# Passing from attention to the experts: the expert counts' own PSUM bank, weight splits moved behind the masked copies, the second item's rows turned earlier, and the second expert cut into items of 2 and 4 tiles

## The chip, the cores and the metric

The program runs on one core of one Trainium2 chip. Its engines are TensorE (PE, with its weight loads shown apart as PEld), VectorE (DVE), ScalarE (ACT), GpSimd (POOL) and SyncE (SP, which here only issues transfers). Each engine works through its own queue in order, and semaphores tie the queues together. The metric is the device time of one execution in microseconds (us), as the median of several runs.

## The reference, cut to what matters

A block of a transformer on 4096 tokens of width 256: a layer norm with modulation, windowed attention (16 heads of 64, window 128), a gated residual, a second modulated layer norm, and a mixture of experts with top-2 routing, 8 experts of width 1024 and a capacity of 640 rows per expert and choice.

```python
h = _layernorm(x) * (1 + ca) + sa
x = x + ga * attention(h, Wqkv, Wout)          # window of 128 keys, 16 heads
h = _layernorm(x) * (1 + cb) + sb
probs = softmax(h @ gate_w.T + gate_b);  topk_prob, topk_idx = top_k(probs, 2)
for c in range(2):                              # each choice
    pos = cumsum(one_hot(topk_idx[:, c]))[own] - 1
    keep = pos < 640                            # capacity
    xb = rows of h, put to slot (expert, pos)
    yb = relu(xb @ W1 + b1) @ W2 + b2           # per expert
    y += yb[slot] * prob * keep
x = x + gb * y
```

All of it is float32. The kernel keeps that precision by splitting each operand into a high and a low part in a reduced format and adding three products (`passes`, line 227).

## The kernel before, in words

**Attention.** The tokens are taken in 16 groups of 256 (`NG`), and the heads in 8 pairs. A software pipeline (`iteration(w)`, line 1084, for w = 0 to 66) does two head pairs in each step: scores of step w, softmax of step w-1, transposes (`turn`, `unpack`) and value products of step w-2, output projection of step w-3. On all five engines the order of instructions is exactly the order in which the program text emits them (`tc.manual_schedule`, line 1157). Within an iteration there are named places, in this order: A, B, M, H, C (ahead of the scores), S (after the scores' masked copies, `pack`), V (after the value products). Side work is hung on these places: the string "2B" in a list means "two iterations after the base, at place B".

**Close.** When a group's projection is complete, `close(g)` (line 633) does the residual, the second norm, the routing, and puts the rows into their slots in a DRAM buffer `xbuf` with four indirect transfers from POOL (line 819, "puts"). It is a generator of eleven pieces: 1 residual, 2 statistics, 3 the normed rows `h` (two adders on POOL, or on DVE for the last group), 4 transposes `tp_f`, 5 logits `pl`, 6 and 7 the two picks (7 ends with the running counts `pref`), 8 the position counts `cnt`, 9 weights, 10 ranks, 11 slot numbers and the puts. `CLOSE`, `LATE` (lines 1031 to 1036) say where each piece of a group is hung. In the last two groups (14 and 15) piece 8 also computes the rows an expert has so far (`totals`, line 737), by a matmul into free columns of the same PSUM bank as `cnt`. From it comes `shift`, which pushes the late rows of experts 0 and 1 behind row `EARLY` = 512, so that the rows ahead of it can be read back before the late puts are done.

**Experts.** The rows of an expert are in tiles of 128, ten tiles per expert at most. An item is a run of tiles of one expert: expert 0 has items 0 to 4 with 2 tiles each; expert 1 has item 5 with 4 tiles and items 6 to 8 with 2; then an item of 6 tiles and two of 2 for each further expert. For an item, `load_slots` reads rows from `xbuf` by a transfer on SP (line 870); `turn_slots` transposes them on PE (`tp_x`, line 895) and splits them on ACT and DVE into `xT` (line 127); `first_layer` and `second_layer` are the matmuls `ph` and `y` for each of 8 slices f of the hidden width, with `hm` made from `ph` by one ACT and two DVE instructions (lines 937 to 939); `y` runs two slices behind. `results` and `give` add the rows into the output by indirect transfers (line 1003). Weights of an expert come in four pieces (`Expert.steps`): load, then a split on ACT and DVE (`we`, line 127).

**The passage.** Items 0, 1, 5 and 2 bridge the two parts. Item 0 (expert 0) is woven into iterations 62 to 66. Item 1 follows with the last pieces of close(15) between its slices. Then comes item 5, which covers the time until the last puts are in DRAM and read back for item 2. Item 2 is the first that the tile scheduler orders itself. After it, items 3 and 4 run only if expert 0 has more rows than 6 tiles (`further`, a branch on all engines), then item 6, then items 7 and 8 under the same kind of branch, then item 9 with 6 tiles of expert 2. With these inputs expert 0 keeps 675 rows and expert 1 keeps 686, so items 3, 4, 7 and 8 are skipped.

The side work that the change touches was hung so:

```python
NG - 3: ["0H", "1A", "1B", "2B", "2H", "3A", "3B", "3H", "3C", "3C", "3C"],      # group 13
NG - 2: ["0H", "1A", "1B", "2B", "2H", "2C", "3A", "3B", "3M", "3C", "3C"],      # group 14
place(experts[0].pieces, NW - 4, "0A 2B 2C 3B 3C".split())     # NW = 64
place(experts[1].pieces, NW - 1, "0B 1B 1C 2M 3A".split())
place(first, NW - 2, "0A 1H 1S 2B 2H 2V 3B 3H 3V 4A".split())  # item 0
```

Of the kernel before, what the change touches and what calls it, by code (L numbers as in the profile page):

```python
# [8 lines left out]
FP = mybir.dt.float32  # L9
FR = mybir.dt.float32r  # L10
I32 = mybir.dt.int32
AF = mybir.ActivationFunctionType
ALU = mybir.AluOpType
# [4 lines left out]
P = 128  # L18
# [10 lines left out]
def adaln_block_kernel(  # L29
# [18 lines left out]
    nc = tc.nc  # L48
# [4 lines left out]
    E, _, FF = w1.shape  # L53
    CAP = 640
    KC = 2
    BUF = KC * CAP
    NSLOT = E * BUF
    T = B * S
    NT = T // P
    ND = D // P  # L60
    NP = H // 2
    NF = FF // P
    NB = BUF // P
    SBT = 2
    NG = NT // SBT
# [2 lines left out]

    EARLY = 4 * P
    WIDE = 6
    QSCALE = DH ** -0.5

# [16 lines left out]
    def bank(name, shape=(P, 512)):  # L91
        return ring["pool"].tile(list(shape), FP, tag="ring", name=name, bufs=ring["bufs"])
# [7 lines left out]
    ones = const.tile([P, P], FP, name="ones")  # L100
# [5 lines left out]
    shift = const.tile([P, 2], FP, name="shift")  # L106
# [215 lines left out]
    first = norm(0)  # L322
# [310 lines left out]
    def close(g):  # L633
# [3 lines left out]
        j0 = g * SBT  # L637
# [96 lines left out]
        n = SBT * KC * E  # L734
        ohf = oh.rearrange("p t k e -> p (t k e)")

        def totals(j, o):

            nc.tensor.matmul(
                out=cnt[:, o : o + KC * E], lhsT=ones,  # L740
                rhs=pref[:, j, :, :].rearrange("p k e -> p (k e)"), start=True, stop=True,
            )
            both = small.tile([P, KC, E], FP, tag="both", name=f"both_{g}_{o}", bufs=2)
            nc.vector.tensor_scalar(
                both.rearrange("p k e -> p (k e)"), cnt[:, o : o + KC * E], float(CAP), None, ALU.min
            )
            total = small.tile([P, E], FP, tag="total", name=f"total_{g}_{o}", bufs=2)
            nc.vector.tensor_tensor(total, both[:, 0, :], both[:, 1, :], ALU.add)
            return total

        if late:

            e = g - (NG - 2)
            total = totals(j0, n)
            nc.vector.tensor_scalar(
                shift[:, e : e + 1], total[:, e : e + 1], -1.0, float(EARLY), ALU.mult, ALU.add
            )
            nc.vector.tensor_scalar(shift[:, e : e + 1], shift[:, e : e + 1], 0.0, None, ALU.max)
        nc.tensor.matmul(out=cnt[:, 0:n], lhsT=tri, rhs=ohf, start=True, stop=False)
        nc.tensor.matmul(  # L760
            out=cnt[:, 0:n], lhsT=ones,
# [2 lines left out]
        )  # L764
        counts = small.tile([P, n], FP, tag="counts", name=f"counts_{g}", bufs=2)
        nc.vector.tensor_copy(counts, cnt[:, 0:n])
        yield
        sm = tile2("sm")
        nc.vector.tensor_reduce(sm, ex, AX.X, ALU.add)
# [32 lines left out]
        nc.vector.tensor_scalar(over, rank, float(CAP), float(2 * NSLOT), ALU.is_ge, ALU.mult)  # L802
        rows_of = NSLOT
        if late:
            rows_of = NSLOT - EARLY
            for e in range(g - (NG - 2) + 1):
                sel = tile2("sel", SBT * KC)
                nc.vector.tensor_scalar(
                    sel, pk, float((E - e) * P), shift[:, e : e + 1], ALU.is_equal, ALU.mult
                )  # L810
                nc.vector.tensor_tensor(pos_, pos_, sel, ALU.add)
# [19 lines left out]
                placed.append(put)  # L831
        if g == NG - 1:

            total = totals(NT, n)
            nc.vector.tensor_tensor(total[:, 0:2], total[:, 0:2], shift, ALU.add)
            nc.vector.tensor_copy(fill, total)

# [3 lines left out]

    items = []
    for e in range(E):
        head = 2 if e == 0 else 4 if e in (1, E - 1) else WIDE
        ends = [0, *range(head, NB + 1, 2)]
        items += [(e, range(lo, hi)) for lo, hi in zip(ends, ends[1:])]
    NI = len(items)
    xts, xTs, hms, yps, b2s = {}, {}, {}, {}, {}
# [28 lines left out]
    def turn_slots(q, n0):  # L877

        tiles = items[q][1]
        if n0 == 0:  # L880
            w = len(tiles)
            if q and (w > 2 or items[q - 1][0] in (1, E - 1) and items[q - 1][1].start == 0):
                w = WIDE
            xTs[q] = [
                (mp if q else early).tile([P, ND, w * P], FR, tag=f"xT{i}{w}", name=f"xT{i}_{q}")
                for i in range(2)
            ]
        m = min(2, len(tiles) - n0)
        if m <= 0:
            return  # L890
        tp = bank(f"tp_x{q}_{n0}")
        tpv = tp.rearrange("p (d s) -> p d s", d=ND)
        for n in range(m):
            for d in range(ND):
                turned = nc.tensor.transpose(
                    tpv[:, d, n * P : (n + 1) * P], xts[q][:, n0 + n, d * P : (d + 1) * P], ident
                )
                if q > 6:
                    tc.keep_in_program_order(turned)
        s = slice(n0 * P, (n0 + m) * P)  # L900
        split(xTs[q][0][:, :, s], xTs[q][1][:, :, s], tpv[:, :, 0 : m * P])
# [96 lines left out]
    def give():  # L998
# [31 lines left out]
    NORM = ["0B", "1A", "1H", "2A", "2B"]  # L1030
    CLOSE = ["0H", "1A", "1B", "2H", "3H", "4A", "4B", "5H", "6A", "6B", "6C"]
    LATE = {
        NG - 3: ["0H", "1A", "1B", "2B", "2H", "3A", "3B", "3H", "3C", "3C", "3C"],
        NG - 2: ["0H", "1A", "1B", "2B", "2H", "2C", "3A", "3B", "3M", "3C", "3C"],
        NG - 1: ["0H"],
    }
    places = {}
# [1 line left out]
    def place(work, w, at):  # L1039
        for a in at:  # L1040
            places.setdefault((w + int(a[0]), a[1]), []).append(work)
# [28 lines left out]

    experts = {e: Expert(e) for e in range(2)}
    first = first_item()
    place(experts[0].pieces, NW - 4, "0A 2B 2C 3B 3C".split())
    place(experts[1].pieces, NW - 1, "0B 1B 1C 2M 3A".split())
    place(first, NW - 2, "0A 1H 1S 2B 2H 2V 3B 3H 3V 4A".split())

    def go(w, at):
        for work in places.pop((w, at), ()):
            next(work, None)
# [4 lines left out]
    def iteration(w):  # L1084
        g, p2 = divmod(w, NP // 2)
        if p2 == NP // 2 - 1 and g + 2 < NG:
            xs[g + 2] = load_x(g + 2)
        for i in range(2 * w - 2, 2 * w):
            if 0 <= i < E:
                clear(i)  # L1090
        new, old, turned, done = pair(w), pair(w - 1), pair(w - 2), pair(w - 3)

        ahead = [divmod(i, NP // 2) for i in range(w + 1, NW if w == NW - 3 else w + 2) if i < NW]
        if w == NW - 2:
            ahead = []
        if w == NW - 2:
            project_v(g, 1, 1)
        if turned[0]:
            turn(*turned[0])
            unpack(*turned[0])  # L1100
        if old[0]:
            normalize(*old[0])
        go(w, "A")
        q = [project_qk(*a, 0) for a in ahead[:1]]
        if old[1]:
            exps(*old[1], [0])
        for a in q:
            part(*a)
        if turned[1]:
            turn(*turned[1])  # L1110
        if old[1]:
            exps(*old[1], [1, 2])
        if turned[1]:
            unpack(*turned[1])
        if old[1]:
            exps(*old[1], [3])
        go(w, "B")
        k = [project_qk(*a, 1) for a in ahead[:1]]
        if old[1]:
            normalize(*old[1])  # L1120
        for a in k:
            part(*a)
        for a in ahead[1:]:
            for i in range(2):
                part(*project_qk(*a, i))
        if done[0]:
            out_project(*done[0])
        if w < NW:
            for a in VALUES[p2] if g + 1 < NG else LAST_VALUES[p2]:
                project_v(g, *a)  # L1130
        go(w, "M")
        if done[1]:
            out_project(*done[1])
        go(w, "H")
        go(w, "C")
        for u in new:
            if u:
                scores(*u)
        if new[0]:
            pack(*new[0])  # L1140
            maximum(*new[0])
            pack(*new[1])
        go(w, "S")
        if turned[0]:
            values(*turned[0])
        if new[0]:
            maximum(*new[1])
            exps(*new[0], [0, 1])
        if turned[1]:
            values(*turned[1])  # L1150
        if new[0]:
            exps(*new[0], [2, 3])
        go(w, "V")

    part(*project_qk(0, 0, 1))
    everything = {mybir.EngineType.PE, mybir.EngineType.Activation, mybir.EngineType.DVE, mybir.EngineType.Pool, mybir.EngineType.SP}
# [4 lines left out]

    next(last)
    next(first)
    next(last)
    next(first)
    next(first, None)
# [4 lines left out]
    mp = ctx.enter_context(tc.tile_pool(name="moe", bufs=2, reuse_waits="tile"))  # L1171
    pm_ = ctx.enter_context(tc.tile_pool(name="pmoe", bufs=1, space=PSUM, reuse_waits="tile"))
    ring.update(pool=pm_, bufs=2)
    load_slots(1)
    load_slots(5)
    load_b2(1)
    turn_slots(1, 0)
    second = layers(1)
    for f in range(NF + LAG + 1):
        next(second, None)  # L1180
        next(last, None)
        if f in (6, 8):
            turn_slots(5, f - 6)
    load_slots(2, 2)
    load_slots(6, 2)
    third = layers(5)
    for f in range(NF + LAG + 1):
        next(third, None)
        if f == 0:
            give()  # L1190
        if f == 6:
            turn_slots(2, 0)
    order.__exit__(None, None, None)

# [24 lines left out]
    def do(f, *a):  # L1219
        return lambda: f(*a)  # L1220
# [24 lines left out]
                further(q + 1)  # L1245

    filled = []
    item(2, {0: [give], 3: [fills], 4: [do(turn_slots, 6, 0)], 6: [do(turn_slots, 3, 0)]})
    further(3)
    more = {f: [do(piece, 2)] for f in (0, 2, 4, 6)}  # L1250
    more[1] = [do(load_slots, 9)]
    more[7] = [do(turn_slots, 7, 0)]
    for i in range(3):
# [43 lines left out]
```

## Time and profile before

| what | value |
|---|---|
| median of 3 runs | 1161.58 us (1160.19 to 1163.09) |
| profiled execution, its own time | 1161.56 us |
| its span in the trace | 1159.8 us |
| PE busy | 1086.3 us (94%) |
| DVE busy | 877.4 us (76%) |
| ACT busy | 676.7 us (58%) |
| POOL busy | 593.8 us (51%) |
| mean granted TensorE clock | 0.97 |

The page's second part cuts the span into 40 slices of 29 us each and gives a digit for every engine, tenths of busy time. Its row PEclk is the clock granted to TensorE in the same tenths. In a timeline each row is a run of like instructions: start, duration, engine, line and operation, the tile written and those read, the count, and in brackets how long the engine was idle just before and which instruction or transfer released it.

### The profile page before, as it was taken

How to read it: one execution, taken by the hardware profiler on the slowest of the kernel's cores; microseconds unless marked ns; L12 is line 12 of the kernel's file. 1: busy time of each engine (PE TensorE's matmuls, PEld its weight loads, DVE VectorE, ACT ScalarE, POOL GpSimd, SP SyncE). 2: the span in 40 equal slices, each digit the busy share in tenths (PEclk: the TensorE clock that was granted, in tenths of full speed). 3: DMA queues.
4: the chain of work that ended last, by engine and by line, in shares of the span. 5: the costliest groups of instructions: out<-in, count | busy, mean ns of one | idle time of the engine just before them, and what ended most of it. 6: DMA issues, size and time to landing. Idle time of an engine off the chain costs nothing. (4 is left out here: it accounts for less than half of the span.)

```text
span 1159.8 us, 25187 instructions
## 1 busy us (share of the span) xinstructions
PE 1086.3 (94%) x9246; PEld 999.6 (86%) x9246; DVE 877.4 (76%) x2168; ACT 676.7 (58%) x2097; POOL 593.8 (51%) x769
## 2 busy tenths in 40 slices
PE   6799999999999999999999997779889999999995
PEld 4678999999999888999999896768879999999995
DVE  6556688888878778888878877767667777878764
ACT  4467776777777567777777676423344444344441
POOL 4235465665675556665675665433522615443524
PEclk9899999999999999999999998879989999999998
DMA  6890010010010010010010022233432524342413
GB/s 228 194 218 21 1 39 19 21 39 19 21 39 19 21 43 29 21 36 20 17 37 20 18 65 70 85 91 95 83 106 87 84 84 90 83 89 67 83 45 36
DMA packets 59571, 72.09 MB, mean 62 GB/s; under 512 B 4807, under 2 KB 51152, under 8 KB 59436
## 3 DMA queue, kind: packets, MB, share of 16 engines
q1 hardware_dynamic: 36988, 44.27, 12.2%
q0 software_dynamic: 11712, 14.79, 7.4%
q10 hardware_dynamic: 10736, 11.27, 4.3%
q8 instruction: 80, 1.31, 0.5%
q14 instruction: 55, 0.45, 0.1%
HBM read 40.11 MB, written 32.27 MB: 62 GB/s over the span
## 5 line engine op out<-in xcount | busy, mean ns | idle before, releaser
L937 ACT ACTIVATE hm<-ph,b1T 128x256 fp32r<-128x256 f32 (+2 forms) x184 | 99.3, 540 | 224.8 <-PE ph L232 192.6
L232 PE MATMUL pq<-hh,wq 128*128 128x256 f32 x1024 | 216.8, 295 | 3.5 <-ACT hh L268 3.0
L232 PE MATMUL ph<-xT,we 128*128 128x256 f32 (+2 forms) x1104 | 203.6, 325 | 15.5 <-DVE xT L127 4.6
L550 ACT ACTIVATE pm<-pm,mx 128x128 f32<-128x128 f32 x512 | 204.1, 402 | 19.4 <-DVE mx L536 16.7
L232 PE MATMUL y<-we,hm 128*128 128x256 f32 x1440 | 201.5, 285 | 6.6 <-DVE hm L939 6.6
L232 PEld LDWEIGHTS y<-we,hm 128*128 128x128 f32 x1440 | 186.7, 190 | 10.7 <-DVE hm L939 9.3
L232 PEld LDWEIGHTS ph<-xT,we 128*128 128x128 f32 x1104 | 172.3, 196 | 21.2 <-issue 6.5
L584 POOL TENSOR_SCALAR_AFFINE_SELECT pT<-pT 128x512 f32<-128x512 f32 (+1 forms) x128 | 80.9, 632 | 211.6 <-ACT pT L583 211.5
L232 PEld LDWEIGHTS pq<-hh,wq 128*128 128x128 f32 x1024 | 170.0, 193 | 5.8 <-ACT hh L268 3.4
L938 DVE TENSOR_SCALAR r<-ph,b1T 128x256 f32<-128x256 f32 (+2 forms) x184 | 101.8, 562 | 73.1 <-ACT hm L937 65.6
L560 POOL TENSOR_TENSOR pm<-pm,rd 128x512 f32<-128x512 f32 x128 | 133.8, 1045 | 28.5 <-DVE rd L558 26.4
L232 PE MATMUL pq<-hl,wq 128*128 128x256 f32 x512 | 145.8, 285 | 0.0
L526 ACT COPY pm<-sc 128x256 f32<-128x256 f32 (+1 forms) x256 | 80.6, 363 | 107.9 <-PE sc L502 70.3
L1002 POOL TENSOR_TENSOR ys<-ys,gw 128x256 f32<-128x256 f32 x56 | 48.4, 971 | 175.7 <-DVE ys L992 157.0
L607 PE MATMUL av<-pT,v 128*64 128x128 f32 (+1 forms) x1472 | 126.7, 321 | 4.7 <-POOL pT L588 2.2
L607 PEld LDWEIGHTS av<-pT,v 128*64 128x64 f32 x1472 | 91.1, 140 | 33.7 <-POOL pT L588 4.6
L1003 POOL DMA_INDIRECT out_dram<-ys,tok x60 | 98.1, 1634 | 33.5 <-issue 11.4
L527 DVE COPY_PREDICATED pm<-within,sc 128x256 f32<-128x256 int32 (+1 forms) x256 | 96.1, 422 | 22.0 <-ACT pm L526 21.1
L502 PE MATMUL sc<-kr,qh 64*128 64x256 f32 (+1 forms) x1024 | 105.7, 296 | 5.0 <-DVE ql L300 2.0
L550 ACT ACTIVATION_READ_ACCUMULATOR pm<-pm,mx 128x1 f32 x512 | 99.6, 194 | 0.0
L232 PEld LDWEIGHTS pq<-hl,wq 128*128 128x128 f32 x512 | 99.0, 193 | 0.0
L939 DVE TENSOR_TENSOR hm<-r,hm 128x256 fp32r<-128x256 f32 (+2 forms) x144 | 94.6, 657 | 5.3
(162 smaller groups left out, 2261.9 us busy)
## 6 DMA issues: line engine op xcount, KB each, us to landing
raw_w<-in_L_ffn_W_dram SPq DMA_DIRECT2D x32, 512.0 KB, 3.9
xbuf<-blank ACTq DMA_DIRECT2D x16, 685.0 KB, 9.6
xt<-xbuf SPq DMA_DIRECT2D x8, 822.0 KB, 4.9
x<-in_L_attn_x_dram SPq DMA_DIRECT2D x16, 256.0 KB, 2.8
out_dram<-x SPq DMA_DIRECT2D x16, 256.0 KB, 2.3
xt<-xbuf SPq DMA_DIRECT2D x7, 548.0 KB, 5.0
raw_wq<-in_L_attn_Wqkv_dram SPq DMA_DIRECT2D x6, 512.0 KB, 7.0
wm<-in_L_wmod_dram SPq DMA_DIRECT2D x1, 1024.0 KB, 11.1
```

Of the source, the lines that this page charges most:

```text
L232: nc.tensor.matmul(out=out_, lhsT=a, rhs=b, start=start and n == 0 and i == 0, stop=stop and n == last and i == 2, **kw,)
L502: nc.tensor.matmul(out=sc[h][:, t, lo:], lhsT=q[r, t * P : (t + 1) * P], rhs=kr[r, (0, 1, 0)[i], hp, blk, :], start=(i == 0), stop=(i == 2),)
L526: nc.scalar.copy(pm[:, h, ts, :], blocks[:, own, :])
L527: nc.vector.copy_predicated(pm[:, h, ts, :], within.rearrange("p (a k) -> p a k", a=1).to_broadcast([P, n, P]), blocks[:, before, :],)
L550: nc.scalar.activation(pm[:, h, t, :], pm[:, h, t, :], AF.Exp, bias=mx[:, h, t : t + 1], accum_out=den[:, h, t : t + 1],)
L560: nc.gpsimd.tensor_tensor(pmv, pmv, rd.rearrange("p h (t a) -> p (h t) a", a=1).to_broadcast([P, 2 * SBT, P]), ALU.mult,)
L584: nc.gpsimd.affine_select(out=pT[:, :, t0:, 0, :], in_=own[:, :, t0:, :], pattern=[[0, 2], [0, n], [-1, P]], compare_op=ALU.is_gt, fill=0. ...
L607: nc.tensor.matmul(out=av[h * DH : (h + 1) * DH, q0 : q0 + hi - lo], lhsT=v[:, f0 + h * DH : f0 + (h + 1) * DH], rhs=pT[:, h, lo:hi], star ...
L937: nc.scalar.activation(hh[:, s], phv, AF.Relu, bias=bias)
L938: nc.vector.tensor_scalar(r[:, s], phv, bias, 0.0, ALU.add, ALU.max)
L939: nc.vector.tensor_tensor(hl, r[:, 0:W], hh, ALU.subtract)
L1003: add = nc.gpsimd.indirect_dma_start(out=of, out_offset=bass.IndirectOffsetOnAxis(ap=tok[:, 0:1], axis=0), in_=y, in_offset=None, bounds_c ...
```

## The change

`totals` takes a PSUM bank of its own from the ring, and its matmul comes after the two `cnt` matmuls and the copy `counts`, where it stood ahead of them. `EARLY` becomes a pair, 512 rows for expert 0 and 256 for expert 1. The second expert's items become 2, 4, 2 and 2 tiles (items 5 to 8), so item 5 has half the tiles and item 6 twice as many. The pieces of groups 13 and 14, of the weights of experts 0 and 1, and of item 0 are hung on other places; several weight splits move from B and C to S and V, behind the masked copies. Item 1's rows are read at the end of iteration 64 (they were read after iteration 66) and turned ahead of the last slice of item 0, into tiles taken from the pool of the attention's input rows `x`. The reads of items 6 to 8 are separate (4 tiles, then 2+2).

```diff
-    EARLY = 4 * P
+    EARLY = (4 * P, 2 * P)
...
-        def totals(j, o):
+        def totals(j, name):
+            tot = bank(f"tot_{name}")
             nc.tensor.matmul(
-                out=cnt[:, o : o + KC * E], lhsT=ones,
+                out=tot[:, 0 : KC * E], lhsT=ones,
...
-        if late:
-            e = g - (NG - 2)
-            total = totals(j0, n)
-            nc.vector.tensor_scalar(shift[:, e : e + 1], total[:, e : e + 1], -1.0, float(EARLY), ALU.mult, ALU.add)
-            nc.vector.tensor_scalar(shift[:, e : e + 1], shift[:, e : e + 1], 0.0, None, ALU.max)
         nc.tensor.matmul(out=cnt[:, 0:n], lhsT=tri, rhs=ohf, start=True, stop=False)
...
         nc.vector.tensor_copy(counts, cnt[:, 0:n])
+        if late:
+            e = g - (NG - 2)
+            total = totals(j0, g)
+            nc.vector.tensor_scalar(shift[:, e : e + 1], total[:, e : e + 1], -1.0, float(EARLY[e]), ALU.mult, ALU.add)
+            nc.vector.tensor_scalar(shift[:, e : e + 1], shift[:, e : e + 1], 0.0, None, ALU.max)
...
-        head = 2 if e == 0 else 4 if e in (1, E - 1) else WIDE
-        ends = [0, *range(head, NB + 1, 2)]
+        head = 2 if e < 2 else 4 if e == E - 1 else WIDE
+        ends = [0, 2, *range(6, NB + 1, 2)] if e == 1 else [0, *range(head, NB + 1, 2)]
...
             xTs[q] = [
+                xp.tile([P, ND, w * P], FR, tag="x", name=f"xT{i}_{q}") if q == 1 else
...
-        NG - 3: ["0H", "1A", "1B", "2B", "2H", "3A", "3B", "3H", "3C", "3C", "3C"],
-        NG - 2: ["0H", "1A", "1B", "2B", "2H", "2C", "3A", "3B", "3M", "3C", "3C"],
+        NG - 3: ["0H", "1A", "1B", "2B", "2H", "3A", "3B", "3H", "3C", "3C", "4C"],
+        NG - 2: "0H 1B 1V 2H 2C 2V 3A 3B 3H 3C 3V".split(),
...
-    place(experts[0].pieces, NW - 4, "0A 2B 2C 3B 3C".split())
-    place(experts[1].pieces, NW - 1, "0B 1B 1C 2M 3A".split())
-    place(first, NW - 2, "0A 1H 1S 2B 2H 2V 3B 3H 3V 4A".split())
+    place(experts[0].pieces, NW - 4, "0A 2B 2S 3S 3V".split())
+    place(experts[1].pieces, NW, "0A 0V 1M 1V 2B".split())
+    place(first, NW - 2, "1A 1C 1V 2B 2H 2V 3B 3H 3V 4A".split())
...
         go(w, "V")
+        if w == NW:
+            load_slots(1)
...
     next(last)
     next(first)
+    turn_slots(1, 0)
     next(last)
...
-    load_slots(1)
     load_slots(5)
     load_b2(1)
-    turn_slots(1, 0)
...
-        if f in (6, 8):
-            turn_slots(5, f - 6)
+        if f == 6:
+            turn_slots(5, 0)
     load_slots(2, 2)
-    load_slots(6, 2)
+    load_slots(6)
...
-        if f == 6:
+        if f == 7:
             turn_slots(2, 0)
...
-    item(2, {0: [give], 3: [fills], 4: [do(turn_slots, 6, 0)], 6: [do(turn_slots, 3, 0)]})
+    item(2, {0: [give], 2: [fills], 3: [do(turn_slots, 6, 0)], 5: [do(turn_slots, 6, 2)], 7: [do(turn_slots, 3, 0)]})
     further(3)
     more = {f: [do(piece, 2)] for f in (0, 2, 4, 6)}
+    more[0].append(do(load_slots, 7, 1))
     more[1] = [do(load_slots, 9)]
```

## The prediction

> **What bounds the kernel now.** I read the page's slices first, then the windows around the change, then the PE timeline, and last the other queues at each PE wait.
>
> In the page, PE is busy nine tenths or more nearly everywhere:
>
> ```profile
> PE   6799999999999999999999997779889999999995
> PEclk9899999999999999999999998879989999999998
> ```
>
> PE sets the time, and only in slices 25 to 31 (some 700 to 900 us), the passage to the experts, does it fall to seven or eight tenths, with its clock. The rest of the span is as good as untouched by the change: the instruction orders of all engines agree up to the end of group 13. So the sum is made from this passage. In windows (length, PE, PEld, DVE, ACT, POOL busy, granted clock, DMA share, GB/s):
>
> ```profile
> 705.00:758.00 53.00, 41.26 (x341) 36.51 (x340) 38.37 (x102) 30.77 (x92) 28.26 (x33) 0.87 0.28 88
> 758.00:790.00 32.00, 23.25 (x147) 21.58 (x145) 22.01 (x78) 7.43 (x16) 9.31 (x15) 0.79 0.31 75
> 790.00:831.00 41.00, 35.84 (x252) 33.23 (x253) 27.71 (x51) 13.06 (x25) 22.23 (x24) 1.00 0.35 80
> 831.00:856.00 25.00, 18.52 (x120) 16.90 (x121) 15.04 (x27) 10.28 (x19) 7.91 (x9) 0.85 0.54 149
> ```
>
> PE idles 32 of 151 us here, and low clock stretches what it does. The PE timeline names each wait in brackets:
>
> ```profile
> 709.36 1.09 PE L607 MATMUL av<-pT,v 128*64 128x256 f32 x12
> 712.65 1.97 PE L607 MATMUL av<-pT,v 128*64 128x256 f32 x12 [2.20 <-POOL pT L588]
> ...
> 725.63 1.27 PE L232 MATMUL ph<-xT,we 128*128 128x256 f32 x5 [2.81 <-DVE xT L127]
> ...
> 745.74 0.41 PE L759 MATMUL cnt<-oh,tri 128*128 128x32 f32 x2 [4.39 <-DVE both L744]
> ...
> 764.83 1.12 PE L895 MATMUL tp_x<-ident,xt 128*128 128x128 f32 x4 [4.81 <-DMA xt<-xbuf]
> 767.47 2.16 PE L232 MATMUL ph<-xT,we 128*128 128x256 f32 x6 [1.52 <-ACT xT L127]
> 769.43 1.05 PE L674 MATMUL tp_f<-ident,h 128*128 128x128 f32 x4
> ...
> 781.14 0.41 PE L759 MATMUL cnt<-oh,tri 128*128 128x32 f32 x2 [1.61 <-DVE both L744]
> ...
> 808.10 0.60 PE L895 MATMUL tp_x<-ident,xt 128*128 128x128 f32 x4
> ...
> 830.88 3.52 PE L232 MATMUL ph<-xT,we 128*128 128x256 f32 x18 [3.65 <-PEq L1241]
> 837.85 0.66 PE L895 MATMUL tp_x<-ident,xt 128*128 128x128 f32 x4 [0.72 <-DMA xt<-xbuf]
> ...
> 847.88 0.97 PE L232 MATMUL y<-we,hm 128*128 128x256 f32 x6 [0.95 <-DVE hm L939]
> 849.87 0.73 PE L232 MATMUL y<-we,hm 128*128 128x256 f32 x4 [1.02 <-DVE hm L939]
> ```
>
> See three things: the item-1 rows come 4.81 us late (764.83); after such waits the same work costs more (twelve `av` 1.09, then 1.97); and item 6 (from 830.88) waits for `hm` again and again.
>
> **The change, part by part.** Call T0 the end of the last attention projection on PE, 758.4.
>
> *Up to T0.* Moving the puts of group 13 from iteration 61 to 62 frees POOL: they took 703.1 to 707.9 ahead of the selects of `pT`, so `av` waited 2.20. That wait goes. But their slot numbers now stand on DVE behind the residual (ends 713.1, moved up to 712.7 by what left the queue), so the puts run about 713.2 to 718.3. SP reads item 0's rows 1.5 after the last put (707.94 to 709.44 in the trace) and they land 2.9 later: 722.7. PE reaches their transposes, now ahead of the last scores, at about 717, since its `tp` waits until 714 for a bank that DVE's masked copy frees. So PE idles some 6 us, and the scores begin at 723.4 where they began at 720.0. Against that, the three weight and row splits on DVE (1.21, 0.65, 1.54), which held the masked copies until 726.96, go behind them: copies start at about 726, the 2.81 wait goes, and `av` of iteration 63 ends at 729.2 as against 730. Next late is `h` of group 14: its DVE step is now behind the copies and its two POOL adders (2.09 and 2.05) end at 735.9, where `tp_f` ran at 730.8; PE waits about 2.6. Queued behind the adders on POOL are the selects for `av` of iteration 64, which end at 740 instead of 735.4.
>
> The totals: the wait at 745.74 is put down to `both`, but DVE ended `pref`, which `cnt` needs anyway, at 745.6, and `both` at 745.69. The own bank buys 0.2 there and 0.7 at 781.14, not 4.39. Only one weight split (1.22) instead of two stands on DVE ahead of `pref` now, but logits come later (738.8 for 737.4): I get `cnt` at 747.2. So T0 comes at about 759.9: **1.5 later**. Bounds: 3 earlier (rows of item 0 are in time) to 6 later (nothing behind the wait absorbs it).
>
> *T0 to the end of item 2.* Before: 758.4 to 827.2, 68.8 us. Item 1's rows are now read two iterations earlier, so 4.81 goes; their split is covered by the last `y`. What is late next is `h` of group 15: DVE ended it 6.2 after T0 (764.6), and `tp_f`, at T0+11.0, moves only to T0+6.3. From there the DVE chain decides: logits +8.7; its two picks (14 small operations of 0.17 to 0.2), two `hm` pairs of 0.9 and `pref` bring `cnt` to +14.8, a wait of 2; `r`, weights, ranks, a row split and slot numbers took 9.1 after that `r` in the trace, here 8.7 as one split is half as large: slot numbers at +24.3, where they were at +31.7 (790.1). Item 5 starts on PE at +23.3.
>
> A pair of slices `ph` and `y` costs 1.43 for two tiles (0.72 + 0.71, rows at 819.6 and 820.3) and 2.81 for four (796.9 to 799.7). Item 5 with two tiles reaches the turn for item 2 after two `ph` and six pairs, 10.0: +33.3. The rows for it: puts of 4 x 1.3 end at +29.5, the read is issued at +30.9 (795.3 to 796.7 before), lands 4.7 to 5.3 later: +35.9. Before, the transposes ran at 808.1, 6 us behind the landing; that cover is gone, and PE waits 2.6. Split 0.6 + 0.7, meanwhile two `y`: item 2 starts at +37.8. Item 6's rows are third in SP's queue (behind item 2's and 548 KB for items 7 and 8) and wait until item 5's row factors have been read; that third read went out 5.5 after the first (802.2), here at +36.4, landing +41.3, needed at +40.0: 1.3. Item 2 takes 8 x 1.43 and 12 transposes of 0.09: +50.3, with the wait 51.6, and I add 1.5 for the clock (below): 53.1. Before, without the two tiles that moved to item 6 (8 x 1.38 = 11.0): 57.8. **4.7 saved.** Bounds: 1 to 8.
>
> *Item 6.* Before, two tiles took 830.88 to 850.6, 19.7 us, for 11.4 of slices and 1.4 of transposes. The 6.9 lost are the clock after the branch (18 `ph` 3.5 instead of 2.2), the waits shown, and ACT: it stood 3.09 in front of a weight load not yet landed, with `hm` behind. Expert 2's four weight pieces are one per two slices; with four tiles they have 5.6 instead of 2.9 us each, so the loads (6.1 to land here) are in time. DVE work in it: 8 x (0.75 + 0.69), 4 x 1.22, 4 x 0.68, 4 x 0.48, 2 x 0.68: 22.4, just under PE's 22.5 + 1.4. With 1.2 for the clock and 0.7 for the last `hm`, 25.8; before plus 11.0 is 30.7. **4.9 saved.** Bounds 2 to 6.5, the lower if DVE, this close, binds.
>
> *At nothing:* the branches (3.65 stays: the same jump); one more read on SP and ACT's load of `fill` moved into item 2 (0.75, ACT half idle there); `EARLY` for expert 1 (it skips the same items); the tiles from the pool of `x` (their last readers end 20 us earlier); `give` of four tiles instead of two after item 6, under item 9's 40 us of PE.
>
> **A rule against the row.** The Trainium skill, TensorE: Matmul & The Clock Gate, Part 1, says that the clock halves after an idle window of about 3.4 us and returns after as long a busy one. Here the 2.20 wait was enough (1.09 to 1.97) and 1.61 was not (the `ph` after it ran at full speed). By the rule the new waits of 2.0 to 2.6 cost nothing further, and the sum is 1.5 better, 1152.0; I take the row.
>
> **Sum:** +1.5 - 4.7 - 4.9 = -8.1. The profiled execution took 1161.56 (1.8 around its span), the median is 1161.58, so the difference carries over: **1153.5**.
>
> **Rivals.**
> 1. *The wait moves behind item 5.* Item 5's cover of 10 us against a put-to-rows chain of 11.6 is the tightest place; if reads take 6.7 as one did here, and item 6's rows are later too, with low clock, this section saves 0.5, and DVE binds item 6 (3): 1.5 - 0.5 - 3 = -2, **1159.6**. For it: three reads at once took 4.7 to 6.7. Against it: sizes in front are no larger than before.
> 2. *Item 0's late rows pass through one to one; slower.* The 6 us wait stands ahead of the last scores, the head of the softmax chain. If the read lands 3 later (822 KB took up to 5.9 where this took 2.9), the clock stays low until the logits as it did from 764.8 to 776 (+5), and `h` adds its 2.6 on top of the 3.4: T0 is 14 later, and -9.6 leaves +4.4: **1166.0**. It decides from a T0 more than 13 later. Against it: copies and splits trade places in just this stretch.
> 3. *It falls better.* Scores no later, T0 2 earlier, 6 and 6 saved: **1147.6**.
> 4. *The totals' bank does what its name says not*: as above, in the sum already.
>
> **How the numbers follow.** What can be told from no change is about 0.3%, 3.5 us. Forecast 0.65 (own range 1149 to 1158), rival 1 0.17, rival 2 0.09, rival 3 0.09. Faster: forecast, rival 3 and a little of rival 1, 0.76; same: most of rival 1, 0.14; slower: 0.10. The range leaves out half of rival 2 and the far end of rival 3: 1146.5 to 1163.5.
>
> **What would show it.** Right: `tp_x` of item 0 waits 4 to 7 us on its rows and the masked copies follow directly; no wait on rows for item 1, but `tp_f` waits on `h` twice; `cnt` still waits on DVE, for `pref`; a wait on rows for item 2; item 6 near 26 us with hardly a wait on `hm`. Wrong: T0 more than 6 us later; item 2's rows in time (more gain) or over 5 us late; item 6 above 28 us.

## The result, and the profile after

The changed kernel takes 1154.98 us (median of 5 runs, 1154.35 to 1156.12). The kernel before took 1163.09 us beside it (5 runs). The ratio is 0.9938, 95% interval 0.9924 to 0.9953: faster, by 7 us by the ratio. The forecast was 1153.5. The profiled execution took 1156.12 us, its span 1154.4; before it was 1161.56 and 1159.8. So between the two traces 5.4 us are to be found.

In the page, PE is at six to eight tenths in five slices of the passage, where five had seven or eight; the last low one comes a slice earlier, and the clock is below nine tenths in two of them, where it was so in four:

```profile
PE   6799999999999989999999998688899999999995
PEclk9889999999999999999999999879999999999998
```

The four windows of the passage (length, PE, PEld, DVE, ACT and POOL busy, granted clock, DMA share, GB/s):

```profile
705.00:758.00 53.00, 37.18 (x304) 32.58 (x306) 33.53 (x91) 28.21 (x88) 26.84 (x32) 0.84 0.31 86
758.00:790.00 32.00, 25.06 (x178) 23.60 (x174) 26.23 (x86) 10.35 (x22) 11.88 (x16) 0.84 0.32 76
790.00:831.00 41.00, 34.48 (x247) 32.06 (x248) 27.24 (x63) 15.95 (x31) 19.69 (x24) 0.96 0.39 98
831.00:856.00 25.00, 23.38 (x162) 21.76 (x161) 18.78 (x28) 11.34 (x19) 6.33 (x7) 1.00 0.48 139
```

The first window got worse (PE 37.2 us busy where it was 41.3), and the last got better (23.4 for 18.5, at full clock). The timeline of PE shows the waits, with the idle time before each row and what ended it in brackets:

```profile
718.05 0.58 PE L232 MATMUL po<-wo,al 128*128 128x256 f32 x1 [1.85 <-DVE al L300]
725.79 1.09 PE L897 MATMUL tp_x<-ident,xt 128*128 128x128 f32 x4 [5.24 <-DMA xt<-xbuf]
738.24 0.66 PE L674 MATMUL tp_f<-ident,h 128*128 128x128 f32 x4 [2.13 <-POOL h L661]
750.05 0.38 PE L752 MATMUL cnt<-oh,tri 128*128 128x32 f32 x2 [3.89 <-DVE oh L721]
767.72 0.88 PE L232 MATMUL ph<-xT,we 128*128 128x256 f32 x5 [2.42 <-DVE xT L127]
770.46 1.11 PE L674 MATMUL tp_f<-ident,h 128*128 128x128 f32 x4 [1.86 <-DVE h L661]
773.64 1.88 PE L681 MATMUL pl<-gwT,h2T 128*128 128x8 f32 x8 [0.79 <-ACT h2T L676]
782.50 0.38 PE L752 MATMUL cnt<-oh,tri 128*128 128x32 f32 x2 [1.15 <-DVE oh L721]
802.99 0.66 PE L897 MATMUL tp_x<-ident,xt 128*128 128x128 f32 x4 [1.31 <-DMA xt<-xbuf]
808.15 1.09 PE L897 MATMUL tp_x<-ident,xt 128*128 128x128 f32 x8 [0.95 <-DMA xt<-xbuf]
822.59 5.96 PE L232 MATMUL ph<-xT,we 128*128 128x512 f32 x18 [3.71 <-PEq L1244]
```

The wait for item 1's rows (4.81) is gone. Item 0's rows are 5.24 us late ahead of the last scores. `tp_f` waits twice for `h`, and a slice of item 1 waits 2.42 for its split rows `xT`. The two waits at `cnt` are still there, and DVE's `oh` ends them. Item 6, from 822.59, has no wait on `hm`.

**The passage in sections.** To compare kernels I divide each trace at points that all have. The start is `cnt` of group 13: no instruction differs up to there, and it still comes anywhere from 699.0 to 702.7 us, so its place is a spread of runs and not an effect. T0 is the end of the last attention projection on PE, as in the prediction. The end is the first `y` of item 9; from there to the end of the span all the kernels take 300.7 us within 0.2. All times in us; where the items are as before, item 2's section holds the two tiles (11.0) that the changed kernel moves to item 6. The second column says how item 0's rows are put and read (an iteration early, as in the kernel before, or late) and where their four transposes stand in iteration 63.

| kernel | item 0's rows, turn | start to T0 | T0 to end of item 2 | item 6 | from there to `y` of item 9 | whole passage |
|---|---|---|---|---|---|---|
| before | early, ahead of scores | 58.7 | 68.6 | 19.6 | 8.7 | 159.4 |
| changed | late, ahead of scores | 62.0 | 55.8 | 25.8 | 5.3 | 152.7 |
| item cut alone | early, ahead of scores | 58.7 | 58.8 | 25.7 | 4.5 | 152.0 |
| all but the item cut | late, ahead of scores | 62.2 | 65.0 | 18.7 | 9.4 | 159.5 |
| turn behind the values | late, behind values | 58.1 | 55.8 | 25.8 | 6.9 | 150.4 |
| two factor buffers | late, ahead of scores | 62.5 | 55.3 | 25.8 | 5.0 | 152.6 |
| item 1's rows late | late, ahead of scores | 62.1 | 57.1 | 26.5 | 4.8 | 154.6 |
| totals in the counts' bank | late, ahead of scores | 64.0 | 56.2 | 25.9 | 5.0 | 154.9 |
| totals first, in that bank | late, ahead of scores | 63.0 | 57.4 | 26.9 | 4.7 | 155.9 |
| last split late | late, ahead of scores | 62.0 | 60.9 | 26.7 | 6.8 | 160.4 |
| old places | early, ahead of scores | 60.5 | 54.4 | 26.8 | 5.0 | 150.4 |
| old places, new splits | early, ahead of scores | 58.2 | 55.4 | 25.8 | 4.9 | 148.6 |
| old places, two buffers | early, ahead of scores | 58.4 | 52.5 | 25.8 | 4.8 | 145.7 |
| values, two buffers | late, behind values | 59.9 | 55.2 | 25.8 | 4.9 | 149.9 |

The branch of about 4 us between item 2 and item 6 belongs to the whole only. The column from start to T0 falls into two groups: 62.0 to 64.0 wherever late rows are turned ahead of the scores, 58.1 to 60.5 elsewhere.

### The profile page after: what moved, and what is told of

It is laid out like the page before. It is cut to its first block, busy times and chain, and to the rows that moved or that the text cites. A ratio compares the mean times of both kernels' runs of the same rounds, so it can differ in the third digit from the quotient of the medians.

```text
span 1154.4 us, 25197 instructions
## 1 busy us (share of the span) xinstructions
PE 1078.9 (93%) x9246; PEld 991.9 (86%) x9246; DVE 876.5 (76%) x2168; ACT 677.6 (59%) x2097; POOL 592.8 (51%) x769
## 3 DMA queue, kind: packets, MB, share of 16 engines
q8 instruction: 80, 1.31, 0.5%
## 5 line engine op out<-in xcount | busy, mean ns | idle before, releaser
L232 PE MATMUL ph<-xT,we 128*128 128x256 f32 (+2 forms) x1104 | 198.1, 320 | 9.7 <-PEq L1244 3.7
L232 PEld LDWEIGHTS ph<-xT,we 128*128 128x128 f32 x1104 | 167.7, 191 | 15.0 <-issue 5.1
L232 PE MATMUL po<-wo,ah 128*128 128x256 f32 x512 | 98.3, 285 | 0.0
```

Of the source, the lines that this page charges most:

```text
L232: nc.tensor.matmul(out=out_, lhsT=a, rhs=b, start=start and n == 0 and i == 0, stop=stop and n == last and i == 2, **kw,)
```

## The experiments

Each ran in five rounds against the kernel before on the same chip. Three chips were used; the kernel before had medians of 1162.2, 1162.4 and, for the last four kernels, 1165.3 us, so those four are judged by ratio and by section, and not by bare time.

**1. The item cut alone.** The kernel before with nothing but the cut of the second expert.

```diff
-        head = 2 if e == 0 else 4 if e in (1, E - 1) else WIDE
-        ends = [0, *range(head, NB + 1, 2)]
+        head = 2 if e < 2 else 4 if e == E - 1 else WIDE
+        ends = [0, 2, *range(6, NB + 1, 2)] if e == 1 else [0, *range(head, NB + 1, 2)]
```

> The kernel before with only the items of the second expert cut into 2, 4, 2, 2 (reads and turns moved with them), nothing else of the change. Theory A (the items carry the gain: item 6 saves 4.8 us in the trace, the wait and low clock after the next branch 3.5, and item 5's shorter cover costs 1 to 3): 6 to 7 us below the kernel before, a ratio near 0.994 to the kernel before. Theory B (the gain comes from item 1's rows being early, and the items only move waits about): within 2 us of the kernel before, and the saving of item 6 is paid back behind item 5.

Measured: 1155.8 us, ratio 0.9951 (0.9937 to 0.9964): 6.4 us by the medians and 5.7 by the ratio, so theory A. Reads and turns of the rows move with the items here and in run 2, as in the change.

**2. All but the item cut.** The changed kernel with the items as before: the first experiment's diff backwards.

```diff
-        head = 2 if e < 2 else 4 if e == E - 1 else WIDE
+        head = 2 if e == 0 else 4 if e in (1, E - 1) else WIDE
```

> The changed kernel with the second expert's items put back to 4, 2, 2, 2. Theory A: it loses 6 to 7 us and stands level with the kernel before (ratio 0.998 to 1.002): the rest of the change nets nothing, since T0 comes 3.3 later and the stretch after T0 saves about as much. Theory B: it keeps most of the gain, ratio 0.994 to 0.996.

Measured: 1161.87 us, ratio 1.0002 (0.9994 to 1.001). The two together bound the share: added to the kernel before, the cut brings 0.49%, 5.7 us; taken from the changed kernel, it costs 0.64%, 7.4 us. So it is most or all of the 7 us, and the rest of the change nets nothing by itself (theory A). The table says why it nets nothing: T0 comes 3.5 later, and T0 to item 2's end is 3.6 shorter. The pair in `EARLY` and the tiles from the pool of `x` were not undone by themselves; both are part of that rest here.

**3. Item 0's turn behind the value products.** The changed kernel with the turn moved off the path of the scores, and the first slice of item 0 with it to the head of the next iteration.

```diff
-    place(first, NW - 2, "1A 1C 1V 2B 2H 2V 3B 3H 3V 4A".split())
+    place(first, NW - 2, "1A 1V 2A 2B 2H 2V 3B 3H 3V 4A".split())
```

> The changed kernel with item 0's rows turned behind the value products of iteration 63 instead of ahead of its scores, and its first slice at the head of iteration 64. Theory A (the 5.24 us wait for rows stands ahead of the last scores and passes through to T0): the wait is gone, the scores start at about 721 instead of 726.8, T0 comes 3 to 4 earlier, and the kernel is 3 us faster than the changed one, ratio to the kernel before 0.991. Theory B (the queues of DVE and POOL behind it, the adders of h above all, set the end of this stretch): T0 moves by less than 1.5, ratio 0.993 to 0.994.

Measured: 1151.79 us, ratio 0.9918 (0.9904 to 0.9931). PE's timeline of this kernel, at the turn and the next wait:

```profile
725.27 0.63 PE L897 MATMUL tp_x<-ident,xt 128*128 128x128 f32 x4 [1.55 <-DMA xt<-xbuf]
742.59 0.52 PE L752 MATMUL cnt<-oh,tri 128*128 128x32 f32 x2 [3.89 <-DVE oh L721]
```

The rows come no earlier than they did (26.3 after `cnt` of group 13, where it was 24.8). PE has its scores and value products done by then, so 1.55 of the 5.24 are left, at full clock (0.63 for 1.09). T0 is 3.9 earlier (theory A). The wait on item 0's rows was the cost. Of the 3.9, 2.3 reach the end of the passage; the stretch behind item 6 is 1.6 longer here.

**4. Two buffers for item 0's row factors.** ACT's factors `gw` of item 0 share one buffer, and the second of them stands in ACT's queue ahead of the copy `h2T` of the last group. ACT's timeline of the changed kernel:

```profile
772.25 0.51 ACT L975 ACTIVATE gw<-gbr,xt 128x256 f32<-128x256 f32 x1 [6.97 <-POOL ys L1004]
773.02 0.57 ACT L676 COPY h2T<-tp_f 128x512 f32<-128x512 f32 x1
```

```diff
-        gw_ = pool.tile([P, D], FP, tag="gw", name=f"gw_{q}_{n}", bufs=6 if q else 1)
+        if q:
+            gw_ = pool.tile([P, D], FP, tag="gw", name=f"gw_{q}_{n}", bufs=6)
+        else:
+            gw_ = wl.tile([P, TS], FP, tag="ah", name=f"gw_{q}_{n}")
```

> The changed kernel with two buffers instead of one for the row factors of item 0 (taken from tiles that are free by then). Theory A (ACT stood 6.97 us in front of the second factor, behind POOL's use of the first, and the copy h2T with the logits stood behind it): the logits of the last group come 1.5 to 2 earlier, item 5 starts as much earlier, but the rows for item 2 come earlier by the same, so all of it is gained: 1.5 to 2 us, ratio 0.992. Theory B (PE at low clock and the DVE queue set it): less than 0.7 us, ratio 0.9935.

Measured: 1154.06 us, ratio 0.9935 (0.9922 to 0.9949), not to be told from the changed kernel (theory B). ACT's 6.97 wait does go, and PE's 0.79 at `pl` with it, but T0 to item 2's end is only 0.5 shorter: `tp_f`, ahead of `pl`, still waits 1.58 on `h`.

**5. Item 1's rows read and turned late**, as before the change.

```diff
-        if w == NW:
-            load_slots(1)
...
-    turn_slots(1, 0)
...
+    load_slots(1)
     load_slots(5)
     load_b2(1)
+    turn_slots(1, 0)
```

> The changed kernel with item 1's rows read and turned where the kernel before does it. Theory A (the wait for h of group 15 stands in the same stretch, so the early rows only replace one wait by another): the 4.8 us wait for rows is back, the two waits of 2.4 and 1.9 go, T0 to item 5 gets 3 to 5 longer, ratio to the kernel before 0.997. Theory B (the early rows are the main gain, with the clock): 7 us or more lost, ratio 0.999 or above.

Measured: 1158.43 us, ratio 0.9973 (0.9959 to 0.9986): 3.5 us slower than the changed kernel by the medians, 4 by the ratios (theory A's size), 1.9 in the traces' passages. The wait comes back, longer than before:

```profile
771.99 1.09 PE L896 MATMUL tp_x<-ident,xt 128*128 128x128 f32 x4 [6.56 <-DMA xt<-xbuf]
```

Of these 6.56 us only 1.3 reach item 2's end: the chain through the last group's `h` runs on meanwhile, and the waits of 2.42, 1.86 and 0.79 at `xT`, `tp_f` and `pl` are gone, with 1.10 at `xT` in their place.

**6. Totals in the counts' bank, behind the counts.** Only the bank is undone; the order stays.

```diff
-            tot = bank(f"tot_{name}")
+            tot, o = (cnt, n)
```

> The changed kernel with the totals back in the bank of cnt (their order behind the counts kept). Theory A (PE waits at cnt for DVE's running counts, not for the bank): 0 to 1 us, ratio 0.993 to 0.9945. Theory B (the bank is what the waits at cnt were about): 3 to 5 us lost, ratio 0.997.

Measured: 1158.87 us, ratio 0.9971 (0.9962 to 0.998). This is no clean undo: the totals' matmul now has to wait for DVE's copy of the counts out of the same bank, waits of 0.28 and, in the last group, 0.68 that neither the kernel before nor the changed one has:

```profile
752.12 0.61 PE L740 MATMUL cnt<-pref,ones 128*128 128x16 f32 x2 [0.28 <-DVE counts L759]
```

The number is theory B's, its reason is not shown: the wait at `cnt` itself stays at 3.90 on `oh`, so it is not the bank that PE waits for there. The two new waits make 1.0. T0 comes 2.0 later in the trace, 1.8 of it behind that `cnt`, where PE now runs at half speed for some 6.6 us and in the changed kernel for 3.4. Whether the bank does that or another draw of the clock is open, and with it the rest of the 3.8 us by the ratios. To price bank and order as they were before, run 7 was made.

**7. Totals first, in the counts' bank.** Bank and order both undone.

```diff
+        if late:
+            total = totals(j0, g)
...
         nc.tensor.matmul(out=cnt[:, 0:n], lhsT=tri, rhs=ohf, start=True, stop=False)
...
         nc.vector.tensor_copy(counts, cnt[:, 0:n])
-        if late:
-            total = totals(j0, g)
```

> The changed kernel (1155 us) with the totals back in the bank of the position counts and back ahead of them, bank and order both as before; all else stays changed. Theory A: PE waits there for the DVE instruction that ends pref, not for the bank, so only the extra matmul and its DVE work stand in the way again: 0.2 to 1 us slower, 1155.2 to 1156. Theory B: the loss of the earlier run with the totals in that bank behind the counts (+3.7 by ratio) came from the shared bank itself: then 1158 to 1159 here too. Theory C: the totals' own bank is what saved the wait shown before: 1159 to 1161.

Measured: 1159.32 us on the chip where the kernel before takes 1165.25, ratio 0.9955 (0.9938 to 0.9971), 0.17% or 2 us above the changed kernel's ratio, with overlapping intervals. PE's timeline of this kernel:

```profile
752.12 0.64 PE L760 MATMUL cnt<-oh,tri 128*128 128x32 f32 x2 [4.18 <-DVE both L745]
786.47 0.41 PE L760 MATMUL cnt<-oh,tri 128*128 128x32 f32 x2 [2.18 <-DVE both L745]
```

The two waits are 4.18 and 2.18 on `both` where the changed kernel has 3.89 and 1.15 on `oh`: the bank and the order are worth 0.3 and 1.0 us there. The wait of 4.39 in the trace of before was DVE's `pref` and `oh` for all but a few tenths, and that speaks against theory C. The time does not decide: the bare 1159.3 lies in C's range, but on a chip where the kernel before is slower too, and the 2 us by the ratios lie between A and B.

**8. Old places.** The changed kernel with the lists for groups 13 and 14, both experts' splits and item 0 as before; of the five lists, the last:

```diff
-    place(first, NW - 2, "1A 1C 1V 2B 2H 2V 3B 3H 3V 4A".split())
+    place(first, NW - 2, "0A 1H 1S 2B 2H 2V 3B 3H 3V 4A".split())
```

> The changed kernel with the places of the pieces as in the kernel before (close of groups 13 and 14, weight splits of experts 0 and 1, item 0); all else changed. Theory A (the new places cost 3.3 us up to T0, by the wait for item 0's rows and by what stands behind it): 2 to 4 us faster than the changed kernel, ratio 0.991. Theory B (the old waits of 2.20, 0.90 and 2.81 with their low clock come back on top of a chain that is no shorter): 1 to 3 slower, ratio 0.995.

Measured: 1150.73 us, ratio 0.9906 (0.9891 to 0.992). The new places cost more than they bring (theory A). The execution in the trace was the slowest of the five, 1153.39, so its sections in the table are rather long.

**9. Old places, but the splits on their new ones.** Against run 8 it parts the splits behind the masked copies from the other moves.

```diff
-    place(experts[0].pieces, NW - 4, "0A 2B 2C 3B 3C".split())
-    place(experts[1].pieces, NW - 1, "0B 1B 1C 2M 3A".split())
+    place(experts[0].pieces, NW - 4, "0A 2B 2S 3S 3V".split())
+    place(experts[1].pieces, NW, "0A 0V 1M 1V 2B".split())
```

> The changed kernel with the places of groups 13 and 14 and of item 0 as before, and only the weight splits of experts 0 and 1 on their new places. With all old places the changed kernel took 1150.7 (ratio 0.9906 to the kernel before). Theory A: the splits behind the masked copies are worth nothing by themselves, and what costs in the new places is item 0's turn ahead of the scores: 1150 to 1152. Theory B: the splits behind the copies gain what they were moved for (the 2.8 us that PE waited for the copies): 1147 to 1149. Theory C: the last weight split ahead of the residual of group 15 costs its 1.2 us and the low clock behind it: 1152.5 to 1154.

Measured: 1150.44 us where the kernel before takes 1165.25, ratio 0.9871 (0.9855 to 0.9888). The bare time fits theory A, the ratio theory B, and they are from different chips. In the traces, start to T0 is 58.2, and the two runs with all old places have 60.5 and 58.4 for the same order of PE's instructions up to there. So a gain of the splits up to about 2 us is possible and not shown. What is excluded is C: they don't cost.

**10. The last split of the second expert later**, behind the normed rows of the last group, since in the changed kernel it stands in DVE's queue ahead of the last residual:

```profile
763.34 1.22 DVE L127 TENSOR_TENSOR we<-raw_w,we 128x1024 fp32r<-128x1024 f32 x1
764.48 0.68 DVE L647 TENSOR_TENSOR h<-po,rows 128x512 f32<-128x512 f32 x1
```

```diff
-    place(experts[1].pieces, NW, "0A 0V 1M 1V 2B".split())
+    place(experts[1].pieces, NW, "0A 0V 1M 1V".split())
...
         next(last, None)
+        if f == 7:
+            next(experts[1].pieces, None)
```

> The changed kernel with the last weight split of expert 1 moved from iteration 66 to slice 7 of item 1. Theory A (in the changed kernel the residual of the last group starts on DVE 1.55 after T0, behind this split, where it started 0.25 after it): h of group 15 comes 1.2 earlier and with it the rest, ratio 0.9925. Theory B (other instructions decide when the logits come): below 0.5 us, or a loss if the split now stands ahead of the slot numbers, ratio 0.994 to 0.995.

Measured: 1161.23 us, ratio 0.9993 (0.9982 to 1.0004): a miss. The counts of the last group do come 1.3 earlier after T0, but item 2 ends 5.1 later, a loss that neither theory had:

```profile
804.62 0.86 PE L897 MATMUL tp_x<-ident,xt 128*128 128x128 f32 x4 [3.35 <-DMA xt<-xbuf]
```

The next expert's weight load goes out on SP behind this split, at 794.0, just ahead of the reads for item 2, whose rows are now waited for 3.35 in place of 1.31: from the first of these reads to the turn it takes 6.5, where it took 4.7. The clock falls behind that wait; the eight `y` after it take 2.06, against 1.19 for eight at full speed. That the load is what holds the rows back was only argued; no run took it away.

**11. Old places and two factor buffers.** The edits of runs 4 and 8 together.

```diff
+    place(first, NW - 2, "0A 1H 1S 2B 2H 2V 3B 3H 3V 4A".split())
...
+            gw_ = wl.tile([P, TS], FP, tag="ah", name=f"gw_{q}_{n}")
```

> The changed kernel with all places as before and with two buffers for the row factors of item 0 instead of one. Theory A: ACT's wait for the single buffer stands ahead of the copy of the transposed rows of group 15 here too, so the two add: 1150.7 less 1 to 2, 1149 to 1149.7. Theory B: with the old places that wait is off the path: 1150.5 to 1151.

Measured: 1147.26 us where the kernel before takes 1165.25, ratio 0.9856 (0.9835 to 0.9877): the fastest kernel of the study, ahead of both. Its gain over run 8 is 3.5 by the bare times, 5 by the ratios and 4.7 in the passages; of the last, 2.1 lie ahead of T0, where both do the same, and 1.8 between T0 and the end of item 2. There PE has no wait at `pl` and none at the last `cnt`, where run 8 waits 0.79 and 0.37; it stands 16.8 after T0 (18.2 in run 8, 19.6 in the changed kernel):

```profile
761.03 0.98 PE L232 MATMUL ph<-xT,we 128*128 128x256 f32 x6 [1.48 <-DVE xT L127]
763.75 1.12 PE L674 MATMUL tp_f<-ident,h 128*128 128x128 f32 x4 [1.74 <-DVE h L661]
765.94 1.71 PE L681 MATMUL pl<-gwT,h2T 128*128 128x8 f32 x8
774.35 0.37 PE L752 MATMUL cnt<-oh,tri 128*128 128x32 f32 x2
```

In the passage that the buffer bears on, it thus seems to pay more here than in run 4 (1.8 for 0.5); why is not shown.

**12. The turn behind the values and two factor buffers.** The edits of runs 3 and 4 together.

```diff
+    place(first, NW - 2, "1A 1V 2A 2B 2H 2V 3B 3H 3V 4A".split())
...
+            gw_ = wl.tile([P, TS], FP, tag="ah", name=f"gw_{q}_{n}")
```

> The changed kernel with item 0's turn behind the value products of its iteration (alone 1151.8, ratio 0.9918) and two buffers for its row factors (alone 1154.1, ratio 0.9935). Theory A: both act after each other, T0 3.9 earlier and item 2 some 0.5 to 1 earlier: 1150.5 to 1151.5. Theory B: the earlier turn gives the factors' buffer back in time, so the second adds nothing: 1151.8.

Measured: 1155.6 us where the kernel before takes 1165.25, ratio 0.9916 (0.9901 to 0.993), beside 0.9918 for the turn alone. As in run 4 the buffer adds nothing that can be told, so theory B's outcome holds, but not its reason: without the second buffer ACT still waits 6.96 at `gw` in run 3.

## Why the prediction was right, point by point

Against the trace of before the forecast was -8.1 in span, and -5.4 was measured: up to T0 +3.3 (the start itself another +1.2), T0 to item 2's end 55.8 against 57.6, -1.9 (the 68.6 of before without 11.0), item 6 -4.8, and behind it -3.4. Item 6 was forecast by mechanism and number. Both sections up to item 2's end fell short of the forecast, by 1.8 and 2.8, and a term behind item 6 that the forecast did not have made good 3.4 of it. That the sum came out so near is luck in that part.

**Up to T0: +1.5 forecast, +3.3 measured.** The step as such held: puts behind the residual, item 0's rows late, PE idle ahead of the last scores. The forecast wait was some 6 us and 5.24 was found, `tp_f` waits 2.13 where 2.6 was forecast. The first of these fits by chance, since both of its ends came late: counted from the start of the passage, PE was free for the rows 2.4 later than forecast and the rows came 1.9 later. Two terms were too small. One is the step "SP reads item 0's rows 1.5 after the last put":

```profile
718.81 0.97 POOL L820 DMA_INDIRECT xbuf<-h,sslot  x1 [0.30 <-issue]
722.93 0.37 SPq L871 DMA_DIRECT2D xt<-xbuf  x1
```

The last put ends on POOL at 719.78 and the read goes out 3.15 later, and then takes its 2.9. SP waits for the puts to land: the four took 4.1 in the median here, and 2.4 in before. This is no spread: in all five kernels with early puts the read goes out 1.5 to 1.6 after the last put, in all nine with late puts 3.0 to 4.5. A weight load of 512 KB goes out at 717.69, in the midst of the late puts; that it delays them is not shown. The other term is the clock, which the sum left at full speed here: the `tp_x` took 1.09 and the scores 2.9, where they took 0.6 and 1.7. Run 3 shows that the wait was avoidable. Rival 2 named this mechanism with the right place and the wrong size: the delay that reached T0 was 3.3, where 13 were needed.

**The `av` wait of 2.20 did not go as a whole.** The forecast let it vanish. PE now waits 1.12 at `av`, for a select on POOL that took 1.64 where most take 0.64; 1.16 at `tp`, for a masked copy on DVE that stands behind the residual and the slot numbers; and 1.85 at `po`, because a weight split of 1.22 on DVE (716.44) stands ahead of the `al` that `po` reads. A wait taken off one queue was found again on the next.

**The totals: right at the two waits.** 0.2 and 0.7 were forecast, 0.3 and 1.0 are what run 7 gives. The wait of 4.39 was DVE's chain, and rival 4 was a fact. What bank and order are worth in the whole time is less clear: 2 us by the ratios, with overlapping intervals.

**T0 to item 2: -4.7 forecast, -1.9 measured.** The logits came at T0+10.7, forecast +8.7; the last `cnt` at +19.6, forecast +14.8; item 2's rows at +40.1, forecast +35.9. The first step that failed is "DVE ended it 6.2 after T0". The residual is not at T0+0.25 as in before but at T0+1.55, behind the weight split shown in run 10, so `tp_f` runs at T0+7.5 and not 6.3. The second is "their split is covered by the last `y`": item 1's split stands on DVE behind that residual and its statistics, and ends at 767.7, so PE waits 2.42 for it. Then the waits of 2.42 and 1.86 leave PE at half speed until about 778: a `ph` of 1.63 and a `pl` of 1.88, against 0.95 and 1.06. The chain from `pl` to `cnt`, 8.9 where 6.1 was forecast, was stretched by PE too, since slices of item 1 stand between them: DVE's picks wait 1.19 for the `hm` of such a slice (at 777.55), a wait that the trace of before has too (at 775.29) and the sum left out. Some came back. Item 5 reached the turn 5.4 later than forecast, the rows only 4.2, so the wait on them was 1.31 and not 2.6, and the clock did not fall behind it: the 1.5 that I added for that were not needed.

**Item 6: -4.9 forecast, -4.8 measured.** 25.8 us, to the tenth, with no wait on `hm`: the weight pieces arrive in time with twice the work over each (ACT's wait of 3.09 on a weight load is gone), and DVE, though close to PE, doesn't bind. The term also survives every edit of the passage (25.7 to 26.9 in all kernels with the new items).

**Behind item 6: nothing forecast, -3.4 measured.** In before, PE waits 0.95 and 1.02 for `hm` at the end of item 6, then 0.84 and 2.04 at the branch into item 9, the last with no releaser shown. The clock is still full for the three matmuls between these two and low after them; the branch in the timelines of before, of the changed kernel and of run 3:

```profile
851.45 0.79 PE L232 MATMUL ph<-xT,we 128*128 128x384 f32 x3 [0.84 <-DVEq L1241]
854.28 5.01 PE L232 MATMUL ph<-xT,we 128*128 128x384 f32 x15 [2.04 <-issue]
...
849.53 0.44 PE L232 MATMUL ph<-xT,we 128*128 128x384 f32 x1 [0.96 <-DVEq L1244]
850.62 3.22 PE L232 MATMUL ph<-xT,we 128*128 128x384 f32 x17 [0.66 <-issue]
...
844.68 4.84 PE L232 MATMUL ph<-xT,we 128*128 128x384 f32 x18 [2.06 <-issue]
```

15 matmuls took 5.01, now 17 take 3.22, and 1.38 of the wait is gone. The two kernels with the old items have 8.7 and 9.4 in this stretch, the twelve with the new ones 4.5 to 6.9, so the items have a part in it. But a wait on `hm` isn't needed for it: run 3 has none in item 6, and PE still stands 2.06 at the branch and is slow behind it. How much of the 3.4 is the items and how much the spread between traces is not shown. The prediction costed item 9 as "under 40 us of PE" and looked no further; without this term the whole would have been a gain of 2 us and not of 5.4. Why PE stands at the branch is open.

**The rule against the row.** For the clock I took the row (a wait of 2.20 halves it) over the Trainium skill, TensorE: Matmul & The Clock Gate, Part 1 (about 3.4 us of idling). Neither was right as I used it. The kernel with only the items cut has the same instructions up to here, waits the same 2.20, and its twelve `av` keep full speed:

```profile
712.96 1.09 PE L607 MATMUL av<-pT,v 128*64 128x256 f32 x12 [2.20 <-POOL pT L588]
715.83 1.97 PE L574 MATMUL tp<-ident,pm 128*128 128x128 f32 x8 [1.79 <-DVE pm L527]
```

There the clock falls one step later. The same page says that the window is free-running, so that the point of change varies with its phase, and the five kernels that have this wait of 2.20 agree: in three the `av` behind it are at half speed, in two they are not. So one row is one draw of several. That 2.20, well under the page's 3.4, can be enough is what the traces show, and the measurement decides. Waits that add up to 4.1 within 8 us (1.12, 1.16, 1.85) also brought the clock down, and a lone 2.13 ahead of `tp_f` did not.

## What to carry to other kernels

Cutting an item smaller where it only covers a wait, and larger where its fixed costs (the loads of weight pieces, the low clock after a branch) are paid, was worth 5.7 to 7.4 us, most or all of the gain, and item 6's part of it held under every other edit. A turn of rows that depends on a chain through DVE, POOL and DRAM should not stand ahead of the work that heads the next chain: behind the value products the same late rows left PE a wait of 1.55 where it had 5.24. Before moving a piece of work off one engine's wait, follow what then stands ahead of the next reader in each queue: here two moved weight splits came to stand ahead of a residual and of an `al`, and the residual ahead of item 1's row split.

## What was not expected of the hardware

With the same order of instructions up to the start of the passage, that start lay anywhere between 699.0 and 702.7 us over 14 traces, and start to T0 took 58.4 and 60.5 in two kernels with equal order there; a term under 2 us can't be read from one trace against another, and several of the terms above are of that size. The kernel before differed by 0.26% between chips (1162.2 and 1165.3 us), as much as most of the terms argued over here. And the branch that skips items 3 and 4 cost PE between 3.8 and 4.3 us in every kernel, whatever the size of the item behind it.
